# One program, two instruction orders: new ordering constants for a fused cross-attention and feed-forward kernel

## The chip, the core and the metric

The kernel runs on one core of one Trainium2 chip. The metric is the device time of one launch in microseconds (us). TensorE (PE in the profile) does the matrix products and writes them to PSUM, VectorE (DVE), ScalarE (ACT) and GpSimd (POOL) do the elementwise work, and all transfers are issued from SyncE's queue (SP). Each engine runs its own instructions strictly in the order in which the program lists them, and waits on semaphores for what other engines produce. So the order of each engine's list is a design choice, and it is the only thing that this change touches.

## The reference, cut to what matters

`x` has the shape (8, 1024, 512), the context (8, 64, 512), all in float32.

```python
# 1: cross-attention with 16 heads of 32, over 64 context rows
q = layernorm(x) @ Wq.T + bq;  k = ctx @ Wk.T + bk;  v = ctx @ Wv.T + bv
q, k = rotate(q, phase), rotate(k, phase)          # one angle per head
x = x + softmax(q k^T / sqrt(32)) v @ Wo.T + bo
# 2: feed-forward: three cycles of a gated twist
y = layernorm(x)
gf = global_net(y.mean(over the 1024 rows))        # 512 -> 256 -> 128 -> 1
out = y
for _ in range(3):
    tf = coupling_net(out)                         # 512 -> 512 -> 256 -> 128 -> 1, gelu, sigmoid
    out = out + (0.1 + ar * (0.7 * gf + 0.3 * tf - 0.5) * 2) * twist(out)
x = x + out
```

## The kernel before, in words

The rows of `x` are cut into 16 halves, (b, h) with b = 0..7 and h = 0..1, of 512 rows each. Attention (`attn_qx`, `attn_half`) goes over the 16 halves, and then the feed-forward (`ffn_load`, `ffn_part`) over 18 parts: 14 whole halves, and the last two halves cut into two parts of 256 rows each. The names of the tiles carry these numbers: `op_3_0_2` is the third output product of half (3, 0), `l2_7_1_2_0` the second layer of the part of half (7, 1) that starts at row tile 2, in cycle 0. The profile leaves the numbers out (`op`, `l`).

What one attention half does on TensorE, in the order of its data: `xp` turns the normalized rows (16 transposes), `qp` is the query product, `sp` the scores from which VectorE takes the row maxima into `mw`, `mp` turns those, `sT` (two of them) makes the scores again and transposed and takes the maxima off by a small product with `hsel`, ScalarE takes the exponential into `pT` and VectorE clamps it, `dn` (two) sums the denominators, their reciprocals go through DRAM and come back spread over the partitions (`rb`), `ap` (two) is the weighted sum of the values, VectorE multiplies it by `rb`, `aT` is its split, and `op` is the output product, which VectorE adds to the rows `xb`. The rows go to DRAM (`x2d`), the second normalization (`xnf`) is turned by VectorE (`tn`) and goes to DRAM too (`xnd`), and its sum is gathered on GpSimd (`acc`) and reduced by the product `gs`.

A feed-forward part loads its turned rows (`fxn`), splits them (`fxT`; GpSimd forms their sum `fs` for the third of them), makes the products `K`, `A`, `B` with the three weights `wg`, and goes three times through the layers `l2`, `l3`, `l4`. The row of gates that `l4` leaves passes through DRAM to be spread (`c0r`, `ber`, `alr`); VectorE forms the next input `f` from the results of `A` and `B`. At the end (`fin`), ScalarE and VectorE form the output rows from `x2d` (`xt`, `x`).

Large float32 products are made as three products of split operands in the type fp32r: "high by high, high by low, low by high" (`mm3`). In this text these are called **split products**. Other float32 products run plain, each as two passes: `sT`, `dn`, `ap`, `gs`, `l4`, and the layers of the last part's cycles 1 and 2. These are called **plain blocks**. The small `hsel` product at the end of an `sT` is of the type fp32r; with its `sT` it is counted here as one plain block.

No instruction is issued while the kernel is written down. Every call is recorded as an operation with an engine, a cost from a small table, its tiles and its dependencies (class `Plan`; `Engine.__getattr__` records, and line 346 issues later, which is why the profile gives line 346 to nearly everything). `Plan.schedule` then fills the engines' lists as a list scheduler: of the operations that are ready on an engine, it takes the one with the lowest priority number for which buffers are free. The number is the place in the source plus offsets from four tables, by the stage's name, its half or part, and its place from the end:

```python
            op.prio = op.n + SHIFT.get(name, 0) + LAST.get(part, 0)
            op.prio += NEAR.get((name, op.unit), 0)
            op.end_prio = op.prio + TAIL.get((name, part), 0)
...
                    key=lambda op: (op.prio if now < FINALE else op.end_prio)
...
                    busy += CHANGE[op.plain] if op.plain != plain else 0.0
```

`CAPS` limits how many buffers of a kind may be in use at once, and so how far ahead a stage may run. PSUM has 8 banks (room `bank`), which all products share, SBUF has rooms of 8 KB (`r8`, one), 4 KB (`r4`, 36) and 2 KB (`r2`, 16) per partition. `tn` and `fxn` share the one room `r8`.

Of the kernel before, what the change touches and what calls it, by code (L numbers as in the profile page):

```python
# [32 lines left out]
DIRECT, DIRECT2 = 2, 6  # L33
POOLED = 99
PLAIN = [(1, 1), (1, 2)]
CAPS = {'xb': 9, 'wn': 5, 'bv': 1, 'bo': 1, 'jm': 1, 'rt': 1, 'kbd': 2, 'vbd': 2, 'pT': 14, 'acc': 76, 'w3': 3, 'w2f': 1, 'w3f': 1, 'h2': 23, 'w4': 1, 'gw2': 1, 'gw3': 1, 'fxn': 2, 'fs': 9, 'f1': 52, 'AB': 35, 'f2': 6, 'f3': 39, 'c': 97, 'x2': 46, 'xe': 23, 'aT': 20, 'wg': 6, 'w2': 2, 'h1': 25, 'xna': 23, 'xnf': 37, 'xT': 5, 'fxT': 23, 'p': 6, 'sp': 75, 'pp': 2, 'ap': 31, 'op': 126, 'qp': 8, 'xp': 1, 'K': 8, 'A': 16, 'B': 65, 'l2': 16, 'l3': 15, 'l4': 57, 'ct': 3, 'qf': 7, 'qr': 1, 'rb': 13, 'mT': 65, 'mw': 1, 'sT': 43, 'mp': 40, 'dn': 1, 'tn': 2}
PARTS = [1, 1, 1, 1, 1, 1, 1, 1, 1, 1, 1, 1, 1, 1, 2, 2]
LAST = {1: 328, 2: -369, 3: -76, 4: 30, 5: -149, 6: -79, 7: -124, 8: 32}
FINALE = 1170
TAIL = {('A', 1): 231, ('A', 2): 300, ('A', 3): -1159, ('A', 4): 2013, ('A', 5): 815, ('A', 6): -359, ('A', 7): 2233, ('A', 8): -1139, ('B', 1): 459, ('B', 2): 757, ('B', 3): -3031, ('B', 4): -117, ('B', 5): 1537, ('B', 6): 39, ('B', 7): -197, ('B', 8): 2457, ('c0', 1): -1522, ('c0', 2): -4, ('c0', 3): -1115, ('c0', 4): -526, ('c0', 5): 10, ('c0', 6): -755, ('c0', 7): -485, ('c0', 8): -1699, ('c1', 1): -3099, ('c1', 2): 2123, ('c1', 3): -1102, ('c1', 4): -1398, ('c1', 5): -3474, ('c1', 6): -3399, ('c1', 7): 1113, ('c1', 8): -1813, ('c2', 1): 1755, ('c2', 2): 715, ('c2', 3): 236, ('c2', 4): 117, ('c2', 5): 2680, ('c2', 6): 92, ('c2', 7): -1348, ('c2', 8): -2522, ('fin', 1): -571, ('fin', 2): 3573, ('fin', 3): -1695, ('fin', 4): -904, ('fin', 5): -559, ('fin', 6): 1080, ('fin', 7): 238, ('fin', 8): -1451, ('load', 1): -1314, ('load', 2): -1153, ('load', 3): 105, ('load', 4): 689, ('load', 5): 1615, ('load', 6): 1287, ('load', 7): -117, ('load', 8): -775}  # L40
NEAR = {('A', 16): -2012, ('A', 17): -2151, ('A', 19): 54, ('A', 20): -891, ('A', 21): -26, ('B', 16): -109, ('B', 17): -240, ('B', 18): -63, ('B', 19): 528, ('B', 20): 34, ('B', 21): 24, ('av', 0): 34, ('av', 1): -205, ('av', 2): -21, ('av', 12): 143, ('av', 13): -5, ('av', 14): -41, ('av', 15): 450, ('c0', 16): -150, ('c0', 18): -1289, ('c0', 20): -5, ('c0', 21): -45, ('c1', 16): 253, ('c1', 17): 92, ('c1', 18): -42, ('c1', 19): -50, ('c1', 20): -240, ('c1', 21): 12, ('c2', 16): -37, ('c2', 18): 356, ('c2', 19): 90, ('c2', 20): -75, ('c2', 21): 16, ('fin', 17): 94, ('fin', 19): -444, ('fin', 20): -52, ('ln1', 0): -466, ('ln1', 1): 104, ('ln1', 2): -29, ('ln1', 13): 75, ('ln1', 14): 45, ('ln1', 15): 618, ('ln2', 0): 135, ('ln2', 1): -30, ('ln2', 2): 331, ('ln2', 14): -256, ('ln2', 15): -328, ('load', 16): -28, ('load', 17): 256, ('load', 18): 427, ('load', 19): -117, ('load', 21): 36, ('m', 0): -389, ('m', 1): 62, ('m', 2): 46, ('m', 12): -74, ('m', 13): 452, ('m', 14): -61, ('o', 0): 398, ('o', 1): 453, ('o', 2): 40, ('o', 12): -97, ('o', 14): -62, ('o', 15): 65, ('pp', 0): -93, ('pp', 1): 222, ('pp', 2): 25, ('pp', 12): -40, ('pp', 13): 63, ('q', 0): 424, ('q', 1): 45, ('q', 2): 88, ('q', 12): 170, ('q', 13): 1286, ('q', 14): 205, ('q', 15): 1677, ('s', 0): -517, ('s', 2): 6, ('s', 12): -85, ('s', 13): -60, ('s', 14): 263, ('s', 15): -38}
SHIFT = {'A': -269, 'B': -2, 'av': -6048, 'c0': -174, 'c1': 49, 'c2': 353, 'fin': 86, 'ln1': -68, 'ln2': -1598, 'load': -314, 'm': 567, 'o': 106, 'pp': -3220, 'q': 495, 's': -6538}


def ts(i, n):
# [83 lines left out]
class Plan:  # L129
# [110 lines left out]
    def schedule(self):  # L240
        ops = self.ops
        for op in ops:
            name, part = op.stage
# [3 lines that stand above are left out]
        engines = sorted({op.engine for op in ops})  # L247
# [4 lines left out]
        while done < len(ops):  # L252
            for e in engines:
                if free[e] > now:
                    continue
                can = [op for op in ready[e] if op.ready <= now]
                can.sort(
                    key=lambda op: (op.prio if now < FINALE else op.end_prio)
                    + (STICK if e == "tensor" and not op.turn and op.plain != plain else 0)
# [132 lines left out]
def tile_xattn_ffn(  # L392
# [31 lines left out]
    def bank(shape, tag, name):  # L424
        return pl.tile("bank", shape, F32, tag, name, CAPS.get(tag, 8), psum=True)

    def t4(shape, tag, name, dtype=F32):
        return pl.tile("r4", shape, dtype, tag, name, CAPS.get(tag, ROOMS4))

    def t2(shape, tag, name, dtype=F32):  # L430
        return pl.tile("r2", shape, dtype, tag, name, CAPS.get(tag, ROOMS2))

# [961 lines left out]
```

## Time and profile before

| | |
|---|---|
| median of 3 runs | 1293.23 us (1292.69 to 1296.7) |
| the profiled execution | 1292.1 us, of which its span from first to last instruction is 1290.3 us |
| busy in the span | PE 1242.7 us, DVE 1047.4, ACT 873.7, POOL 418.6 |
| 60 to 550 us, attention | PE busy 488.48 of 490 us, DVE 352.25, ACT 288.26 |
| 550 to 620 us, passage to the feed-forward | PE 62.99 of 70 us, DVE 59.01, ACT 29.45 |
| 730 to 1160 us, feed-forward | PE 414.27 of 430 us, DVE 391.75, ACT 337.44 |
| 1160 us to the end | PE 115.38 of 131 us, DVE 114.94, ACT 110.71 |

A busy TensorE is not a TensorE at its peak: products are pipelined, so one shows 0.39 us of busy time while the next starts 0.23 us after it. The distance from start to start is what counts for the sum, and it depends on what follows what. The granted TensorE clock stands in the profile as a share of full speed, in stretches of 1.0 and 0.5; over the span it is 0.987.

### The profile page before, as it was taken

Reading aid. Unit: us, or ns where it says so; the run is one execution under the profiler, and the core shown is the slowest. Engines: PE = TensorE matmul, PEld = TensorE weight load, DVE = VectorE, ACT = ScalarE, POOL = GpSimd, SP = SyncE. Lnnn points to the kernel's source line nnn. Section 1 sums busy time; section 2 is a strip of 40 time slices with the busy share of each in tenths; the row PEclk is TensorE's granted clock in tenths of the full one; section 3 lists DMA queues with packets and bytes.
Section 4 is the critical chain, followed back from the end, with each engine's and each line's share of the span. In section 5 each row is a group of like instructions: output and inputs, shape, how many; then the busy total and the mean of one; then the engine's idle time right before and its main releaser. Section 6 shows DMA issues by size and latency. Waiting matters only on the chain. (4 is left out here: it accounts for less than half of the span.)

```text
span 1290.3 us, 21392 instructions
## 1 busy us (share of the span) xinstructions
PE 1242.7 (96%) x7827; PEld 949.9 (74%) x7827; DVE 1047.4 (81%) x1655; ACT 873.7 (68%) x1520; POOL 418.6 (32%) x463
## 2 busy tenths in 40 slices
PE   7999999999999999998999998999999999999996
PEld 6877777676767677756877786777777777778885
DVE  7856877777777776679777989999899996988997
ACT  4574656555566654535657777878778777788897
POOL 4231434334344333304320412313322320334355
PEclk9999999999999999998999998999999999999998
DMA  7312444443444444353430341246534334243445
GB/s 245 123 35 89 126 140 131 135 119 113 121 123 117 139 136 116 92 140 119 145 81 11 111 148 66 80 122 215 169 104 135 113 116 123 74 131 124 160 148 196
DMA packets 163393, 159.05 MB, mean 123 GB/s; under 512 B 88540, under 2 KB 115416, under 8 KB 163288
## 3 DMA queue, kind: packets, MB, share of 16 engines
q1 hardware_dynamic: 163288, 157.69, 40.2%
q8 instruction: 61, 1.00, 0.3%
q14 instruction: 44, 0.36, 0.1%
HBM read 105.62 MB, written 52.03 MB: 122 GB/s over the span
## 5 line engine op out<-in xcount | busy, mean ns | idle before, releaser
L346 PE MATMUL l<-h,w2H 128*128 128x512 f32 (+1 forms) x832 | 245.5, 379 | 5.5 <-DVE h L346 3.9
L346 PEld LDWEIGHTS l<-h,w2H 128*128 128x128 f32 x832 | 150.6, 191 | 37.8 <-DVE h L346 6.2
L346 PE MATMUL l<-h,w2L 128*128 128x512 f32 (+1 forms) x416 | 155.3, 373 | 0.0
L346 ACT ACTIVATE f<-l,bcol 128x512 f32<-128x512 f32 (+1 forms) x162 | 100.6, 637 | 39.7 <-PE l L346 38.6
L346 DVE TENSOR_TENSOR h<-f,h 128x1024 fp32r<-128x1024 f32 x84 | 105.5, 1263 | 11.8 <-ACT h L346 11.4
L346 POOL TENSOR_TENSOR pc<-cc,rs 128x4 f32<-128x4 f32 (+1 forms) x18 | 27.8, 1545 | 262.2 <-DMA cc<-ber 228.8
L346 ACT ACTIVATE xnf<-xb,sm 128x512 f32<-128x512 f32 x64 | 46.0, 720 | 93.3 <-DVE sm L346 88.2
L346 DVE SCALAR_TENSOR_TENSOR xb<-op,xb 128x512 f32<-128x512 f32 x64 | 43.8, 687 | 76.8 <-PE op L346 76.6
L346 POOL TENSOR_TENSOR xb<-xb,bo_b 128x512 f32<-128x512 f32 x64 | 82.9, 1323 | 56.1 <-ACT xna L346 50.3
L346 POOL TENSOR_TENSOR fs<-fxn 128x512 f32<-128x512 f32 x28 | 53.0, 1911 | 142.7 <-PE l L346 73.4
L346 POOL TENSOR_TENSOR acc<-acc,xnf 128x512 f32<-128x512 f32 x64 | 87.7, 1371 | 31.6 <-ACT xnf L346 28.1
L346 ACT CAST h<-f 128x1024 fp32r<-128x1024 f32 x84 | 87.5, 1048 | 10.7 <-PE l L346 4.8
L346 PEld LDWEIGHTS l<-h,w2L 128*128 128x128 f32 x416 | 79.2, 190 | 13.6
L346 ACT ACTIVATE f<-f,bcol 128x512 f32<-128x512 f32 x112 | 76.5, 719 | 16.9 <-DVE f L346 16.5
L346 DVE TENSOR_REDUCE mw<-sp 128x8 f32<-128x512 f32 x128 | 83.7, 680 | 5.1 <-PE sp L346 4.9
L346 POOL TENSOR_TENSOR rs<-rs,mhalf 128x4 f32<-128x4 f32 x16 | 17.2, 1076 | 199.1 <-DVE rs L346 189.9
L346 ACT ACTIVATE pT<-sT 128x512 f32<-128x512 f32 x128 | 66.3, 621 | 10.6 <-PE sT L346 8.2
L346 DVE TENSOR_TENSOR f<-f,A 128x1024 f32<-128x1024 f32 x56 | 70.1, 1255 | 0.4
L346 ACT ACTIVATE xt<-xt,fa 128x256 f32<-128x256 f32 x128 | 65.3, 594 | 6.3 <-DVE fa L346 6.2
L346 ACT ACTIVATE xna<-xb,mb_a,rs_a 128x512 f32<-128x512 f32 x64 | 47.5, 808 | 16.5 <-DVE mb_a L346 16.4
L346 POOL TENSOR_TENSOR rs_a<-rs_a,mhalf 128x4 f32<-128x4 f32 x16 | 22.7, 1420 | 106.9 <-DVE rs_a L346 93.5
L346 DVE TENSOR_SCALAR pT<-pT 128x1024 f32<-128x1024 f32 x64 | 44.2, 699 | 15.9 <-ACT pT L346 15.7
(414 smaller groups left out, 3612.5 us busy)
## 6 DMA issues: line engine op xcount, KB each, us to landing
xb<-in_x_dram SPq DMA_DIRECT2D x32, 512.0 KB
rb<-rd SPq DMA_DIRECT2D x128, 128.0 KB
x2d<-xb SPq DMA_DIRECT2D x32, 512.0 KB
xnd<-tn_f SPq DMA_DIRECT2D x128, 128.0 KB
x<-x2d SPq DMA_DIRECT2D x32, 512.0 KB
xt<-x2d SPq DMA_DIRECT2D x64, 256.0 KB
out_dram<-x SPq DMA_DIRECT2D x32, 512.0 KB
fxn<-xnd SPq DMA_DIRECT2D x28, 512.0 KB
```

Source lines behind the costliest of these rows:

```text
L346: f(*map(real, args), **{k: real(a) for k, a in kw.items()})
```

## The change

Only constants change: `CAPS`, `LAST`, `FINALE`, `TAIL`, `NEAR` and `SHIFT`. No call, tile, cost or dependency of the kernel's source is touched. The shorter tables:

```diff
-LAST = {1: 328, 2: -369, 3: -76, 4: 30, 5: -149, 6: -79, 7: -124, 8: 32}
-FINALE = 1170
+LAST = {1: 202, 2: -902, 3: 253, 4: 25, 5: -160, 6: -84, 7: -123, 8: 28}
+FINALE = 1150
...
-SHIFT = {'A': -269, 'B': -2, 'av': -6048, 'c0': -174, 'c1': 49, 'c2': 353, 'fin': 86, 'ln1': -68, 'ln2': -1598, 'load': -314, 'm': 567, 'o': 106, 'pp': -3220, 'q': 495, 's': -6538}
+SHIFT = {'A': -269, 'B': -2, 'av': -6588, 'c0': -176, 'c1': 49, 'c2': 352, 'fin': -1, 'ln1': -2616, 'ln2': -2261, 'load': -326, 'm': 586, 'o': -898, 'pp': -2635, 'q': 514, 's': -7454}
```

`TAIL` (56 entries) and `NEAR` (82 before, 88 after) get new numbers throughout. In `CAPS`, 34 limits change; among them `xp` goes from 1 to 5, `qr` from 1 to 7, `rb` from 13 to 5, `vbd` from 2 to 1, `fs` from 9 to 1.

Both built programs hold the same instructions on every engine (6536 products and transposes on TensorE, 1591 instructions on VectorE, 1456 on ScalarE, 466 on GpSimd, 759 transfers). 4829 of TensorE's 6536 stand in the same order. The feed-forward's middle is almost untouched: runs of 693, 371 and 602 TensorE instructions, from part (1, 1) to part (6, 0), are the same one after the other, and there the other engines' lists agree as well. What moves is the attention, the passage from attention to feed-forward, and the last three or four parts.

In the attention's steady part, from the first `op` of half (3, 0) to the first `op` of half (4, 0), TensorE's list reads as follows (R: split products; xp, mp: transposes; the other names: plain blocks):

```
before: R | dn | R | dn | R | xp | R | xp | R | xp | R | xp | R | ap ap | mp | R | sT | R | sT | R |
        dn | R | dn | R | xp | R | xp | R | xp | R | xp | R | ap ap | mp | gs | R | sT | R | sT
after:  R | mp | R | sT | R | sT ap ap dn | R | dn | R | xp | R | xp | R | xp | R |
        mp | R | sT | R | sT ap ap dn gs dn | R | xp | R | xp
```

## The prediction

> **What bounds the kernel now.** I read the page first: which engine is busy, and where.
>
> ```profile
> PE 1242.7 (96%) x7827; PEld 949.9 (74%) x7827; DVE 1047.4 (81%) x1655; ACT 873.7 (68%) x1520; POOL 418.6 (32%) x463
> ...
> PEclk9999999999999999998999998999999999999998
> ```
>
> TensorE is busy 96% of the span, and the clock shows only a few dips. The table of windows splits this: attention (60 to 550 us) has 488.48 of 490 us busy, so nothing is to be won there by removing waits, and only the products' spacing can shrink. In the feed-forward TensorE is idle for 4% and VectorE is busy for 91%, so the two share the bound. After 1160 us VectorE is busy for 114.94 of 131 us.
>
> Next, the waits of TensorE over the whole span, longest in total first:
>
> ```profile
> PE B_0p L346 <- DVE fxT L346: 7.9, 5, 3.2
> PE l L346 <- ACT f L346: 7.6, 7, 1.4
> PE l L346 <- DVE h_0L L346: 4.4, 6, 1.4
> PE tr_cT L346 <- POOL dsel L346: 4.3, 1, 4.3
> PE l L346 <- DVE h L346: 3.9, 4, 2.1
> ```
>
> Most are waits for VectorE in the feed-forward, of about a microsecond each. The longest, 3.2 us, is in the passage. All TensorE waits over 0.1 us sum to 35.2 us behind a start at 4.25 us, and 7.9 us follow its last product. The chain that ended last shows only the final 33 us, so I do not use it.
>
> Last, the timeline of TensorE, for what a change of kind costs. First a plain block between split products, then transposes between them (start, duration):
>
> ```profile
> 341.36 0.39 PE L346 MATMUL op<-wo_0L,aT_0H 128*128 128x512 f32 x1
> 341.59 0.40 PE L346 MATMUL op<-wo_0H,aT_0L 128*128 128x512 f32 x1
> 341.92 1.08 PE L346 MATMUL dn<-pT,dsel 128*32 128x128 f32 x32
> 342.93 0.50 PE L346 MATMUL op<-wo_1H,aT_1H 128*128 128x512 f32 x1
> 343.26 0.39 PE L346 MATMUL op<-wo_1L,aT_1H 128*128 128x512 f32 x1
> 343.50 0.39 PE L346 MATMUL op<-wo_1H,aT_1L 128*128 128x512 f32 x1
> ```
>
> ```profile
> 327.90 0.39 PE L346 MATMUL qp<-xT_a_0H,wq_0L 128*128 128x512 f32 x1
> 328.13 0.60 PE L346 MATMUL xp_a<-ident,xna 128*128 128x128 f32 x4
> 328.49 0.48 PE L346 MATMUL qp<-xT_a_1H,wq_1H 128*128 128x512 f32 x1
> 328.80 0.40 PE L346 MATMUL qp<-xT_a_1L,wq_1H 128*128 128x512 f32 x1
> ```
>
> Split products start 0.23 us apart (341.36 to 341.59). The last one before the plain block takes 0.33 (to 341.92), the first one after it takes 0.33 (342.93 to 343.26), and the next 0.24. So each visit to a plain block from split products costs 0.10 + 0.10 + 0.01 = 0.21 us beyond its own work. The durations hide this: 0.39 to 0.50 us overlap.
>
> **Part 1, fewer visits to plain blocks.** In the built order I counted the places where a split product is followed by a plain block, with transposes passed over. Before there are 127, after 104. Up to the first product of the feed-forward it is 73 against 48: in the attention's steady part two halves have 10 visits before and 5 after, because `ap` and `dn` now stand directly behind the second `sT`, and `gs` between two `dn`. In the last stage there are 3 more (22 against 19), and 1 fewer in between. Sum: 23 x 0.21 = 4.8 us. TensorE has no idle time in attention that could swallow it, so it lies on the path.
>
> **Part 2, fewer runs of transposes.** 86 runs before, 57 after. In the second fence four transposes take 0.36 us and the product behind them 0.31 instead of 0.23: 0.44 us for four. In longer runs they start 0.109 us apart, so a run's edges cost little; with the next product's 0.24 it is some 0.03 us per run, 29 x 0.03 = 0.9 us. Bounds: 0 and 1.7 (twice that).
>
> **Part 3, the passage.** Before, `B_0p` waits 3.23 us for the low half of `fxT`, and the clock then falls. The window of the low clock (length, then busy time of TensorE, its weight loads, VectorE, ScalarE and GpSimd, then the mean clock), and the waiting product in the timeline:
>
> ```profile
> 602.48:612.70 10.22, 6.99 (x19) 5.16 (x18) 10.20 (x13) 5.77 (x10) 3.57 (x4) 0.67 0.27 59
> ```
>
> ```profile
> 607.05 0.79 PE L346 MATMUL B_0p<-fxT,wg_2H 128*128 128x512 f32 x1 [3.23 <-DVE fxT L346]
> ```
>
> In these 10.22 us VectorE is busy for 10.20, TensorE for 6.99, at a mean clock of 0.67: 6.8 us at half speed, which cost 3.4 us. After, `K` comes first and `B` last, and all of `op` of half (7, 1) stands ahead. `K` needs the third `fxT` split, VectorE's later one. Counted from the start of the last `ap` (586.92), that split ended at 610.66, 23.7 us later. In the new list VectorE has two additions of 0.61 us to `xb` more ahead of it, and one `wg` split of 0.60 fewer: 24.4. TensorE's own work up to the reading product is, by the same rows, 1.9 (`ap`) + 5.5 (24 `op`) + 4.2 (18 `op`) + 0.9 wait and 0.95 (`gs`) + 6.9 (30 `op`) + 0.2 = 20.6. So a wait of 3.8 us in `K_0p` takes the place of 3.2 us in `B_0p`, with the same work done on either side. The clock decides the rest: -3 us if it does not fall, +4 if it falls and the `B` weights come late too. I take -0.5, near the row of before. Behind the waiting `K` stand `A`, `B` and the first `l2`; nothing else waits for those at that point but VectorE, which is the late one.
>
> This clock rule needs a word. The Trainium skill ("TensorE: Matmul & The Clock Gate", "What's actually happening") says that half clock follows at least one idle window of about 3.4 us. By that rule a wait of 3.8 us may hold no whole window and the passage would gain 3 us. This case's trace speaks against it: half clock followed a wait of 2.04 us at 1110.75, and here one of 3.23.
>
> GpSimd slows VectorE in the same stretch, and I assume it does so after too: two forms of one `w1c` instruction took 0.68 and 1.77 us (both at 599.38 to 601.76) while GpSimd added `fs` from 599.40 to 602.91. The Trainium skill ("Advanced Engine Details and Errata", "Mode Summary") has them block each other on a shared port. The `acc` and `fs` additions stand beside the same weights in the new list.
>
> **Part 4, the last parts.** The order up to some 1160 us is the old one, so its waits stay and everything comes earlier by parts 1 to 3. In the last 130 us all is new. VectorE sat idle for 2.01 us at 1161.6 (gates from DRAM), 1.55 at 1168.4 (a buffer that `l2` of half (5, 1) held) and 1.97 at 1190.5 (`fxT`); the new list finishes that `l2` ahead of the `B` and `K` of the last halves, which can free up to 1.55. The waits of TensorE for `f` there sum to 4.0 us, and the last plain chain stood nearly alone. Now the last two parts end side by side: the two final `l4` are neighbours, so behind the last product ScalarE has 8 `xt` where it had 4. One pass of eight took 4.05 us at 1275.23, so 2.0 us are added. Gains up to 1.55 + 4.0 against losses of 2.0 and more queueing on VectorE: bounds -4 and +5, taken 0, since nothing says which outweighs.
>
> **Part 5, at nothing.** New places of transfers in SP's queue (loads of `xb`, spreads of `rb`, stores of `xnd`): the old trace has no TensorE wait for a transfer in attention, and `dn` to `ap` has 29 us in the new steady part against 22 before. If that cover went, one half would lose what its transfer is late by. The head's reordered transposes fill a wait of 0.78 us for `xna`: at most -0.6, taken 0.
>
> **Sum.** -4.8 - 0.9 - 0.5 + 0 = -6.2 us. The profiled execution took 1292.1 (span 1290.3), 1.1 below the median; -6.2 on it gives 1285.9, on the median 1287.0.
>
> **Rivals.**
>
> *Late VectorE in the joined blocks (slower).* The block `sT ap ap dn` puts four clamps (0.60 each, start to start), four multiplications (0.60), two `aT` splits (1.14) and the reciprocal (0.87) into one burst of 8 us, where before `ap` and `dn` were 4 to 10 us apart. Walking one half by these spacings, the second `dn` has about 1.0 us to spare, the `aT` split 0.95, `mp` 0.5. If VectorE slips past these, each of some 12 halves pays. To be slower by over 0.3%, 10.1 us are needed, 0.84 us in each half. For it: the row of before where this sequence stood without filler (554.9 to 567 us) shows waits of 0.26 to 0.64 us and a fall of the clock. Against it: in attention VectorE is busy for 352 of 490 us, and only 1.3 us of waits for it showed from 60 to 550. Fully paid, at 1 us per half, it gives 1287 + 12 = 1299.
>
> *Given back in the passage and at the end (the same).* `K_0p`'s wait with the clock's fall (+4) or a worse tail (+4) takes back most of 5.7: about 1292.
>
> *The end closes up (faster still).* If the idle time of VectorE at the end goes and TensorE's waits for `f` go with it: -4, some 1282.
>
> *It does not do what it says.* The counts of 127 and 104 are in the built order, so this is excluded.
>
> **Chances.** The forecast, including the closing end, 0.65; given back 0.18; late VectorE 0.17. 0.3% of the time is 3.9 us, about what a measurement of this kernel can tell from no change: faster means below 1289.3, slower above 1297.1. Range: 1278 (all bounds good: -5.7 - 0.8 - 3 - 4 - 0.6 = -14) to 1298 (late VectorE nearly paid in full); about 0.15 lies above and 0.05 below.
>
> **What would show it.** Right: the first `K` product starts some 5 us earlier than 613.67; TensorE's attention windows stay over 99% busy; two halves take 68.5 us where `op` of (3, 0) to (4, 0) took 69.6. Part 3: a wait of 3 to 4 us at `K_0p` instead of `B_0p`, with half clock behind. Part 4: after the last product 10 us instead of 7.9. Wrong: waits `dn <- DVE pT`, `op <- DVE aT` or `mp <- DVE mw` of over 0.8 us in each half, or clock dips inside the attention.

## The result, and the profile after

The changed kernel took 1301.87 us (median of 5 runs, 1299.45 to 1304.96), the kernel before, run beside it, 1294.73 (1292.69 to 1296.75): ratio 1.0052, 95% interval 1.0034 to 1.0071. It is slower, and above the predicted range. The profiled execution took 1302.1 us, its span is 1300.3; that is 10.0 us over the profiled execution of before, which was one of its quicker ones.

The page's line of busy times and the clock row, as shown of before:

```profile
PE 1238.4 (95%) x7827; PEld 958.4 (74%) x7827; DVE 1048.0 (81%) x1655; ACT 874.4 (67%) x1520; POOL 417.5 (32%) x463
...
PEclk9999999999999999999999998999999999898998
```

TensorE is busy for 4.3 us less in a span that is 10 us longer: its products do stand closer, and the time went into waiting. Where, shows in the windows (length, then busy time of TensorE, its weight loads, VectorE, ScalarE and GpSimd, then the mean clock, the DMA share and GB/s), first of before, then of after:

```profile
60.00:550.00 490.00, 488.48 (x3800) 346.89 (x3802) 352.25 (x652) 288.26 (x514) 179.29 (x139) 1.00 0.40 115
1160.00:1290.00 130.00, 115.38 (x788) 102.30 (x786) 114.94 (x221) 110.71 (x246) 58.38 (x76) 0.97 0.49 158
```

```profile
60.00:550.00 490.00, 482.25 (x3863) 352.54 (x3862) 360.66 (x658) 289.97 (x516) 188.42 (x138) 1.00 0.41 114
1160.00:1300.00 140.00, 121.58 (x802) 107.78 (x802) 119.45 (x228) 113.93 (x251) 40.30 (x76) 0.93 0.47 148
```

In the attention TensorE now has 7.8 us of idle time, where it had 1.5. VectorE is busy for 8.4 us more in this window, with six instructions more; 5.4 us of it are five clamps that take longer, shown below. Over the whole span it is busy for only 0.6 us more. At the end the mean clock is 0.93, and it was 0.97. The waits of TensorE, first two rows of before, then the rows of after:

```profile
PE xp_a L346 <- ACT xna L346: 1.1, 2, 0.8
...
PE dn L346 <- DVE pT L346: 0.8, 3, 0.3
```

```profile
PE l L346 <- ACT f L346: 15.7, 7, 3.9
PE l L346 <- DVE h_0L L346: 6.1, 8, 1.4
...
PE dn L346 <- DVE pT L346: 4.0, 6, 0.8
PE xp_a L346 <- ACT xna L346: 3.2, 6, 0.8
PE K_0p L346 <- DVE fxT L346: 2.6, 1, 2.6
PE gs L346 <- POOL acc L346: 2.5, 3, 1.2
...
PE B_0p L346 <- ACT B__12412 L346: 2.1, 1, 2.1
```

The 3.2 us of `B_0p` in the passage became 2.6 us of `K_0p`; the forecast was 3.8. Grown are `dn` and `xp_a` in the attention (4.0 and 3.2 us, from 0.8 and 1.1) and, at the end, the waits for ScalarE.

Start times of the same product in each profile show where a kernel gains and loses (us from the span's start; the rows of the experiments are explained below):

| profile | second `sp` of half (7, 1) | first `B`, part (1, 1) | first `K`, part (7, 0) | end of TensorE | span |
|---|---|---|---|---|---|
| before | 554.9 | 729.4 | 1139.3 | 1282.4 | 1290.3 |
| after | 555.8 | 730.9 | 1143.2 | 1291.4 | 1300.3 |
| s1: new attention, old end | 554.5 | 733.4 | 1143.7 | 1286.9 | 1294.8 |
| s2: old attention, new end | 554.9 | 729.0 | 1142.5 | 1290.4 | 1299.4 |
| b1: new order, short bias addition | 549.6 | 728.9 | 1139.2 | 1285.3 | 1294.2 |
| x2: new order, clamp first | 549.3 | 723.8 | 1135.1 | 1281.8 | 1290.8 |
| s1x2: new attention, clamp first, old end | 549.7 | 723.9 | 1137.2 | 1280.2 | 1288.1 |
| q1: s1x2, sums early in the passage | 549.4 | 730.8 | 1142.2 | 1286.0 | 1293.7 |
| q2: s1x2, sums early at the end | 549.5 | 725.4 | 1133.1 | 1276.3 | 1284.2 |

So the changed kernel arrives at the end of the attention 0.9 us late instead of 5 to 6 early (s1, with the same lists there, 0.4 us early), and from the first `K` of part (7, 0) to the end of TensorE it takes 148.2 us instead of 143.1. Each place has a cause of its own. A row is one execution, so a difference of a few us in one column can be chance; the last section shows two such chances.

**In the attention**, the timeline of the changed kernel around one half (4, 1), VectorE, GpSimd and TensorE in turn:

```profile
376.63 2.37 DVE L346 TENSOR_SCALAR pT<-pT 128x1024 f32<-128x1024 f32 x2
377.04 4.34 POOL L346 TENSOR_TENSOR xb<-xb,bo_b 128x512 f32<-128x512 f32 x3 [1.23 <-ACT xna L346]
379.05 0.64 PE L346 MATMUL dn<-pT,dsel 128*32 128x128 f32 x16 [0.72 <-DVE pT L346]
382.64 0.87 PE L346 MATMUL xp_a<-ident,xna 128*128 128x128 f32 x6 [0.49 <-ACT xna L346]
```

The two clamps of `pT` should take 1.29 us. The second one starts at 377.23, GpSimd's addition of the bias to `xb` 0.19 us before it, and that clamp takes 1.77 us instead of 0.69. The half's second `dn` waits 0.72 us for it, and the next `xp_a` 0.49 us for ScalarE, which had waited for VectorE. The same happens at 170, 239, 308, 377 and 446 us, once in each pair of halves. Before, no clamp of these halves took over 0.70 us; the additions there began behind the last clamp (timeline of before, VectorE and GpSimd):

```profile
308.94 0.69 DVE L346 TENSOR_SCALAR pT<-pT 128x1024 f32<-128x1024 f32 x1
309.95 5.04 POOL L346 TENSOR_TENSOR xb<-xb,bo_b 128x512 f32<-128x512 f32 x4 [1.12 <-ACT xna L346]
```

**At the end**, GpSimd, ScalarE, VectorE and TensorE at 1224 us:

```profile
1216.33 4.18 POOL L346 TENSOR_TENSOR pc<-cc 128x4 f32<-128x4 f32 x2
1222.09 1.40 POOL L346 TENSOR_TENSOR fs__12820<-fxn 128x256 f32<-128x256 f32 x2
1223.53 0.62 ACT L346 CAST fxT<-fs__12820 128x512 fp32r<-128x512 f32 x1 [2.81 <-POOL fs__12820 L346]
1224.18 0.69 DVE L346 TENSOR_TENSOR fxT<-fs__12820,fxT 128x512 fp32r<-128x512 f32 x1 [2.59 <-ACT fxT L346]
1224.57 0.64 PE L346 MATMUL l<-f,w4b 128*32 128x128 f32 x4 [2.69 <-ACT f L346]
```

The sum `fs` of the last part stands behind the 12 small gate instructions of part (6, 1) in GpSimd's list. These have 128 x 4 elements and can take 0.2 us each, but two of them took 4.18 us while VectorE ran one subtraction or addition behind the other. So `fs` is late, then its cast on ScalarE, then everything that ScalarE has behind the cast, then TensorE. Before, this `fs` stood ahead of that group (GpSimd's timeline of before):

```profile
1199.35 1.55 POOL L346 TENSOR_TENSOR fs__12619<-fxn 128x256 f32<-128x256 f32 x2 [9.55 <-DMA fxn<-xnd]
1217.62 10.77 POOL L346 TENSOR_TENSOR pc<-cc,rs 128x4 f32<-128x4 f32 x1 [16.72 <-DMA cc<-ber]
```

There a single gate instruction took even 10.77 us, with VectorE busy without a break beside it, but the last `fs` was done before.

### The profile page after: what moved, and what is told of

It is laid out like the page before. It is cut to its first block, busy times and chain, and to the rows that moved or that the text cites. A ratio compares the mean times of both kernels' runs of the same rounds, so it can differ in the third digit from the quotient of the medians.

```text
span 1300.3 us, 21383 instructions
## 1 busy us (share of the span) xinstructions
PE 1238.4 (95%) x7827; PEld 958.4 (74%) x7827; DVE 1048.0 (81%) x1655; ACT 874.4 (67%) x1520; POOL 417.5 (32%) x463
## 5 line engine op out<-in xcount | busy, mean ns | idle before, releaser
L346 POOL TENSOR_TENSOR xb<-xb,bo_b 128x512 f32<-128x512 f32 x64 | 95.1, 1513 | 75.3 <-ACT xna L346 67.7
L346 POOL TENSOR_TENSOR pc<-cc,rs 128x4 f32<-128x4 f32 (+1 forms) x18 | 9.8, 544 | 281.1 <-DMA cc<-ber 211.8
L346 POOL TENSOR_TENSOR fs<-fxn 128x512 f32<-128x512 f32 x28 | 50.0, 1806 | 143.1 <-DMA fxn<-xnd 76.6
L346 DVE TENSOR_REDUCE mw<-sp 128x8 f32<-128x512 f32 x128 | 81.0, 679 | 2.0 <-PE sp L346 1.9
L346 DVE TENSOR_SCALAR pT<-pT 128x1024 f32<-128x1024 f32 x64 | 48.6, 777 | 21.1 <-ACT pT L346 21.0
L346 ACT ACTIVATE qf<-qp,bqr 128x512 f32<-128x512 f32 x64 | 42.9, 681 | 22.3 <-PE qp L346 21.9
```

What stands on the lines that cost most here:

```text
L346: f(*map(real, args), **{k: real(a) for k, a in kw.items()})
```

## The experiments

**Which part of the order loses?** Both kernels hold the same instructions one after the other in the feed-forward's middle, so the lists can be cut there and joined. The cut is where the sets of what stands before it agree, on every engine:

```diff
+        one, two = self.lists(ONE), self.lists(TWO)
...
+            forced[e] = a[:k] + b[k:]
+        return self.schedule(ONE, forced)
```

> The lists of every engine are those of the changed kernel up to the feed-forward's middle (where both kernels hold the same instructions one after the other) and those of the kernel before from there on. Theory (VectorE and GpSimd block each other, and both ends of the program lose by it): the changed kernel reached the first B product of part (1, 1) at 730.86 us against 729.39 before, so this one should be 1.5 us slower than the kernel before, some 1296, with the clamps beside GpSimd's additions still at 1.77 us. Rival 1 (all of the loss is in the last 130 us and attention is gained as forecast): 5 us faster, 1290. Rival 2 (the attention's waits are the whole loss): 7 us slower, 1302.

Measured: 1296.07 us (median of 12 runs) against 1295.48 (35 runs), ratio 1.0006 (0.999 to 1.0022).

> The reverse: the lists of the kernel before up to the feed-forward's middle, those of the changed kernel from there on. Theory: the end of the changed kernel costs 4.9 us after 1143 us and 1.1 us behind the last product, so 6 us slower than before, some 1301; 9 us if GpSimd is held up at 1102 us again as in the profile of the changed kernel. Rival 1: 12 us slower (the whole loss and the gain of attention with it). Rival 2: no change, 1295.

Measured: 1300.38 us, ratio 1.0041 (1.0021 to 1.0061). So the new end costs 5 us, and the new attention gains nothing. The two effects together, 1.0047, are the changed kernel's 1.0052 within the intervals. Rivals 1 and 2 are both out. In s2's profile the last `fs` was not late (ScalarE waited 0.1 us for it at 1221.6); the long wait there is that of `B_0p` for ScalarE, 3.05 us at 1195, behind another late `fs` (2.5 us). So the row at 1224 us is one form of this loss and not all of it.

**Is it the bias addition beside the clamp?**

```diff
-            pl.gpsimd.tensor_tensor(v, v, bo_b, ALU.add)
+            cut = lambda a: a[:, :8]
+            pl.gpsimd.tensor_tensor(v.via(cut), v.via(cut), bo_b.via(cut), ALU.add)
```

> The changed kernel with GpSimd's additions of the output bias to the rows xb cut to 8 of 512 columns (the rest of the bias is left out), all else in the same order. Theory (the last clamp of every second half stands beside one of these additions and waits for it): the five clamps of 1.77 us fall to 0.69, the waits of dn for pT (0.72) and of xp for xna (0.49) go, which is 1.2 us in each of 6 pairs of halves, so 7 us faster than the changed kernel: some 1295. Rival (the clamp is late because ScalarE's exponentials are, since sT ap ap dn stand in one block): the waits stay, 1302.

Measured: 1296.41 us, ratio to the kernel before 1.0007 (0.9989 to 1.0026). The five clamps fell to 0.69 us, the waits of `dn` for `pT` in the steady halves are gone, those of `xp_a` fell from 0.49 to 0.35, and two halves took 68.03 us (`op` of (3, 0) to (4, 0)) instead of 69.07. The attention's end came 5.3 us earlier than before, but in this profile the first `B` of part (1, 1) only 0.5 us: the passage took the rest, most of it by a lower clock, as the last section shows.

> The kernel before with the same cut, as the control. Theory: no clamp stood beside these additions, and the attention showed 1.3 us of waits for VectorE in all, so at most 1 us faster than before: some 1294. Rival (the additions slow the whole program through their share of the memory): several us faster, as with the changed order.

Measured: 1295.27 us, ratio 0.9995 (0.9979 to 1.0012). In the old order the additions cost nothing, so it is their place in the new order that does. But the edit also shortened GpSimd's work, so the next one only moves it:

```diff
+            def look(col=col):   # ahead of GpSimd's first bias addition of half (b, 1)
+                self.nc.gpsimd.tensor_tensor(self.spare.get(), col.get(), col.get(), ALU.add)
+            op.calls = [look] + op.calls   # col: 4 columns of the last clamped pT of (b-1, 1)
```

> The changed kernel, in which GpSimd reads four columns of the last clamped pT of half (b-1, 1) ahead of its first bias addition of half (b, 1), for the five halves in which the two stood side by side; nothing else moves. So the additions come some 2 us later and behind the clamp. Theory (a lock, not a lack of time: the additions need only begin after the clamp): the five clamps take 0.69 us instead of 1.77, dn waits for pT no more there, two halves take 68.0 us instead of 69.07, as with the shortened additions; the passage takes part of it, so some 1297 in all. Rival (with the additions late, the next wait comes up behind them: xb for op, or rs_a on GpSimd): two halves stay at 69 us or more, 1302.

Measured: 1293.86 us, ratio 0.9983 (0.9964 to 1.0002), where the changed kernel had 1.0052. The timeline of this kernel at the same place (VectorE, GpSimd, VectorE; the file is longer, so the recorded line has another number):

```profile
372.16 1.29 DVE L356 TENSOR_SCALAR pT<-pT 128x1024 f32<-128x1024 f32 x2
373.53 0.20 POOL L323 TENSOR_TENSOR spare<-pT 128x4 f32<-128x4 f32 x1 [2.19 <-DVE pT L356]
373.68 6.99 POOL L356 TENSOR_TENSOR xb<-xb,bo_b 128x512 f32<-128x512 f32 x4
377.22 2.30 DVE L356 TENSOR_TENSOR aT_1L<-rb,aT_1H 128x1024 fp32r<-128x1024 f32 x1
```

Both clamps take 1.29 us together, and GpSimd's additions, all of them still made, wait 2.19 us for them. Two halves take 68.05 us. The additions now hold up a later subtraction instead (`aT_1L`, 2.30 us for 1.21), which TensorE does not wait for. So it is a block and not a lack of time, and what it costs depends on whom it meets. The rival, another wait coming up in its place, is out. The time is some 3 us better than the theory's 1297, which counted on a loss in the passage.

> New attention with the clamp first, from the feed-forward's middle on the lists of the kernel before. Theory: 5 us are gained up to 550 us against the kernel before, the passage gives most of it back, as it did with the shortened additions (there the first B product of part (1, 1) came 0.5 us earlier than before), the end is the old one: 1292 to 1295, no change or just faster than before. Rival (what the passage took was bad luck with the clock, not VectorE): 1290.

Measured: 1289.05 us, ratio 0.9956 (0.9937 to 0.9975). This beats both kernels by more than expected: the passage did not take the gain here (5.5 us at the first `B` of part (1, 1)). It is the rival's number (1290), and the rival's reason, the clock, is borne out by the profiles in the last section. The same program again:

> The best version once more, unchanged. Theory: 0.4 to 0.5% faster than the kernel before, as in its first run. Rival (that ratio was the luck of one chip or of its clock): no difference from the kernel before.

Measured: 1291.71 us against 1294.6, ratio 0.9965 (0.9947 to 0.9983). The gain stands.

**Is the end's loss the wait for GpSimd's sums?**

```diff
-        pl.scalar.copy(xT[0][0], s)
-        low(xT[0][1], s, xT[0][0])
+        near = s.via(lambda a: f32(xT[1][0]).get())
+        pl.scalar.copy(xT[0][0], near)
+        low(xT[0][1], near, xT[0][0])
```

> Old attention with new end, in which the third split fxT is made from the first split's high half instead of from GpSimd's sum fs; GpSimd still forms fs, and the order is the same, so only the wait for GpSimd is taken out (the value of fs is left out of the products K). Theory (the new end loses because its sums fs stand where GpSimd is kept from its port, and ScalarE and TensorE queue behind): the wait of B_0p for ScalarE's B (3.0 us) and the half clock behind it go, and what is left against the old end with the same edit is the 1 to 2 us behind the last product: some 1294. Rival (the order of ScalarE and VectorE is the loss, whoever forms the sum): still 5 us slower than the old end with the same edit.

Measured: 1290.15 us, ratio 0.9963 (0.9947 to 0.9979).

> The kernel before with the same edit, as the control. Theory: the waits of B_0p for fxT (7.9 us in sum) that come from late sums go, at 1110.75 us (2.04 and 1.7 of half clock) above all: 2 to 4 us faster than before, some 1292. Rival: no change, since VectorE is the bound there.

Measured: 1290.61 us, ratio 0.9976 (0.9955 to 0.9997). Without the wait for the sums the new end is no slower than the old one: 1.0041 against 1 became 0.9963 against 0.9976. The wait is the whole loss that the runs can tell. The 1 to 2 us behind the last product that I expected to be left stand in the profiles (9.2 us against 7.9), but not in the medians.

If the place in GpSimd's queue does it, moving the sums alone must help:

```diff
+            held = [
+                i for i, o in enumerate(order[:x])
+                if o in op.deps or any((b.room, b.slot) in slots for b in o.bufs)
+            ]
+            order.insert(max(held) + 1, order.pop(x))   # op: a sum fs; slots: its buffer
```

> The changed kernel, with GpSimd's sums fs of the last two parts moved up in GpSimd's own list: fs of part (7, 1) at row tile 2 from behind the 12 small gate instructions (pc and rc) of part (6, 1) to before them, fs of (7, 1) at row tile 0 three places up. Theory (the new end loses because these sums queue behind small instructions that wait for the port): the idle time of ScalarE and VectorE for fs at 1223.5 us (2.8 and 2.6 us) and TensorE's wait of 2.7 us there with its half clock (1.7 us) go, the wait at 1194.5 shrinks: 4 us faster than the changed kernel, some 1298. Rival (VectorE's backlog at the end is the loss, the sums are late because everything is): no change, 1302.

Measured: 1298.43 us, ratio 1.002 (1.0002 to 1.0037), against 1.0052 for the changed kernel. ScalarE no longer waits for the last part's `fs`; TensorE's waits around 1222 to 1224 us fell from 2.7 to 1.0 us. The wait of `B_0p` for ScalarE's `B` stayed (2.4 us at 1197, 2.1 at 1194 in the changed kernel). It goes the way of the theory and is as large as it said, though the two intervals touch.

> New attention with the clamp first, old end, and in GpSimd's list every fs as early as its loads allow (six parts move, by 2 to 9 places). Theory: in the old end the last sum already stands ahead of the gates, so little is left to gain: 1287 to 1289. Rival (late sums cost the middle too): 1284.

Measured: 1294.99 us, ratio 0.9997 (0.998 to 1.0014): a miss to both sides. The attention still ended early in the profile (549.7 us), but the gain was gone by the first `B` of part (1, 1) (731.4).

> The kernel before with its sums as early as its loads allow (six parts move). Taking the wait for the sums out altogether made it 0.24% faster, which is the most that this can give: 1292 to 1295 by the theory. Rival (GpSimd, ahead in the queue, takes the port from VectorE at worse moments): slower, 1297.

Measured: 1293.63 us, ratio 0.9979 (0.9966 to 0.9992), as the theory said. In the profiles of both, the product `gs` of batch 6 came 3.4 us later behind the `op` ahead of it than without the edit. So the two sums in the passage were tried alone, and then those at the end alone:

> The best version so far (new attention, clamp first, old end) with the sums fs of the first two parts alone moved up in GpSimd's list, the two that stand in the passage. Theory (in the passage GpSimd's additions acc, which the product gs needs, are the more urgent ones; put behind fs they cost what the earlier run with all sums early lost): gs of batch 6 starts 3.4 us later than without the edit, and the whole gain of the attention goes: 1295. Rival (the loss of that run came from the parts in the middle): 1289.

Measured: 1295.87 us, ratio 1.0014 (0.9998 to 1.003). TensorE's longest row of waits in that kernel:

```profile
PE gs L427 <- POOL acc L427: 11.5, 3, 6.8
```

With two sums put ahead of GpSimd's additions `acc`, `gs` waits 11.5 us for them in all, and the gain of the attention goes.

> The best version with the sums of parts (6, 1) and (7, 1) alone moved up. Theory: the gain of 2 to 3 us that the old order had from this edit between 1095 and 1140 us comes on top of the attention's, 1286 to 1288. Rival (the early sums are no gain anywhere): 1289 or later.

Measured: 1287.73 us (median of 7 runs) against 1294.6, ratio 0.9948 (0.993 to 0.9966): the lowest median of all. Its interval overlaps those of the two runs without the early sums (0.9956 and 0.9965), so what these sums add is not shown by the times. In the profile it took 407.6 us from the first `B` of part (1, 1) to the first `K` of part (7, 0), where s1x2 took 413.2. This version has the new attention with five small GpSimd instructions that hold the bias additions back, the old end, and two sums a few places up.

**Is TensorE's longest wait at the end worth anything?** In the changed kernel the last product waits 3.93 us, since ScalarE does 8 `xt` of part (6, 1) first:

```profile
1285.92 4.04 ACT L346 ACTIVATE xt<-xt,fa 128x256 f32<-128x256 f32 x8 [0.17 <-DVE fa L346]
...
1290.38 1.02 PE L346 MATMUL l<-bcol,f 128*128 128x1 f32 x4 [3.93 <-ACT f L346]
...
1291.59 4.26 ACT L346 ACTIVATE xt<-xt,fa 128x256 f32<-128x256 f32 x8
```

```diff
+        late = {o for o in order[:last] if made(o, "xt_6_1_0")}   # and all that depends on them
+        first = [o for o in order[: last + 1] if o not in late]   # last: the second c behind the last l4
+        order = first + [o for o in order if o in late] + order[last + 1 :]
```

> The changed kernel with the last chain (f, and the two c behind the last l4) put ahead of the eight xt of part (6, 1) in ScalarE's list, and these xt with what hangs on them behind it. Theory (at the end ScalarE has 16 xt of 0.49 us to do whatever the order): TensorE's last wait of 3.93 us goes, but the span ends at most 1.2 us earlier, what ScalarE is idle between; no change in the time that can be measured, some 1301. Rival (the wait is on the path): 4 us faster, 1298.

Measured: 1305.05 us, ratio 1.0066 (1.005 to 1.0082). The wait is gone and no time is won; from the last product's end to the span's end it is now 13.9 us instead of 9.0. ScalarE's lines in this kernel:

```profile
1291.08 4.03 ACT L354 ACTIVATE xt<-xt,fa 128x256 f32<-128x256 f32 x8
1296.01 4.28 ACT L354 ACTIVATE xt<-xt,fa 128x256 f32<-128x256 f32 x8 [0.90 <-DVE fa L354]
```

The 16 `xt` set the end, whatever stands ahead of them. Putting the short chain first only leaves ScalarE idle while it waits for TensorE.

## Why the prediction was wrong, step by step

**Parts 1 and 2 (-5.7 us) had the mechanism right; that the size came out so well is partly luck.** With the clamp out of the way the attention ended 5.2 to 5.6 us earlier than before. But two halves took 68.05 us, 1.5 us less than the 69.57 of before, where 1.1 less were forecast (68.5), and they did so with a wait of 0.35 us of `xp_a` still in them. So at the second `sp` of half (5, 1) x2 stood 7.7 us ahead of before, and at that of (7, 1) 5.6: the last halves gave 2 us back, 1.0 of it where that `sp` waits 1.6 us for VectorE's `qr` (0.6 before). The counts hold. Part 2's 0.03 us per run does not come out of its own rows: 0.44 us for four against 4 x 0.109, with 0.01 for the next product, is 0.01 per run, 0.4 us in all.

**What failed first is the sentence that this gain "lies on the path", since TensorE had no idle time to swallow it.** It then made its own: a wait of 0.72 us and one of 0.49 in each pair of halves, and the pair took 69.07 us instead of 68.05. At the second `sp` of half (5, 1) the changed kernel was still 2.3 us ahead of before, at that of (7, 1) 0.9 behind. This is the place of the rival "late VectorE in the joined blocks" but not its mechanism. I looked for a burst too long for VectorE, and gave the second `dn` about 1.0 us to spare. The burst fits; a single clamp came 1.08 us late and `dn` waited 0.72, so the room was 0.36. I had read GpSimd's blocking of VectorE in the passage, from two forms of `w1c` (0.68 and 1.77 us), and did not ask where the new lists put GpSimd's other additions. Part 5 went through SP's queue and left GpSimd's out. Holding the additions back was worth 0.4 to 0.5% in the version with the old end (1.0006 to 0.9956 and 0.9965): this is what had turned the gain into nothing.

**Part 3 (-0.5 us) was near.** The wait moved from `B_0p` to `K_0p` as said, 2.6 us where 3.8 were forecast. From the `gs` of batch 6 to the first `B` of part (1, 1) it took 130.5 us against 129.9, with new waits for GpSimd's `acc` (1.2) and of the product `gp` (1.8). In the other profiles of the new lists it is 131.0 to 133.1 (without q1 and p1, which put the sums ahead of `acc`), in s2 and b2 with the old ones 130.9 and 130.7. By the medians, 131.4 against 130.7, 0.7 us were lost and not 0.5 gained.

**Part 4 (0, between -4 and +5) was mis-sized.** It measured +5 us by the joined lists of s2, the far end of its own bounds. I had listed the idle times of VectorE that could close and the `xt` that could be added, and nothing on GpSimd: that TensorE would wait for a sum behind the gates is not in the working. "Nothing says which outweighs" was not so: the place of `fs` in GpSimd's list was there to be compared. The tail forecast at 10 us after the last product was 9.0.

By measured terms the new attention with the old end is 0.06% or 0.8 us slower, which is the forecast's -5.7 for the spacing and, by subtraction, 6.5 for the clamps, what they hold up and the passage; the new end adds 5.3 (0.41%). That makes 6 us, where 6.7 (0.52%) were measured for both.

Of the signs named ahead, TensorE's attention window is 98.4% busy instead of over 99%, and the row `dn <- DVE pT` is there, but with 0.72 us in every second half, less than the 0.8 in each that was to mean "wrong". The sign of being right came true all the same: the first `K` started at 608.23 us, 5.4 earlier. `K` now stands ahead of `B`, so this start could not tell the gain. Half clock behind `K_0p`'s wait did not come in the changed kernel's profile.

## What to carry to other kernels

When an order changes, compare every engine's list, the idle ones' too: GpSimd was busy for a third of the time and decided the sign here. Some VectorE and GpSimd instructions exclude each other from start to end (here clamps, `aT_1L` and other instructions with two inputs in SBUF), so place GpSimd's work beside VectorE work that nobody waits for, and what another engine needs soon ahead of GpSimd's small gate instructions; but not ahead of what is needed sooner still, as `acc` was. A wait is worth what its end would release: with the 0.72 us of `dn` went 1.0 us of each pair of halves, with the 3.93 us at the end nothing.

## What the runs showed of the hardware

The block works in both directions, and not fairly. A gate instruction on GpSimd of 128 x 4 elements, which takes 0.2 us by itself, took 7.08 us in the changed kernel and 10.77 in the one before, while VectorE went from one two-input instruction to the next without a break; one clamp, the other way round, took 1.08 us more. Not every VectorE instruction is held up: beside the additions at 309.95 us (before) its reciprocal from PSUM took 0.96 us and its addition of a PSUM result 0.68, as elsewhere. The same pair of GpSimd's instructions in the old trace, then in the new one (timeline of before, timeline of after):

```profile
1101.33 0.35 POOL L346 TENSOR_TENSOR pc<-pc,mb 128x4 f32<-128x4 f32 x2
```

```profile
1102.32 7.23 POOL L346 TENSOR_TENSOR pc<-pc,mb 128x4 f32<-128x4 f32 x2
```

The lists are the same there, and all engines are 0.99 us later; presumably it differed which engine got in first, and ScalarE then waited 4.3 us for `fs`. In 12 profiles the instructions and lists are the same here: nine have the 7.08 us, and three (before, s1, b1) have not. From the first `B` of part (1, 1) to the first `K` of part (7, 0) the nine took 411.2 to 413.8 us, the three 409.9 to 410.4. So 1 to 4 us between executions go with this chance, and the profile of before is one of the lucky ones. The Trainium skill ("SBUF — State Buffer", "SBUF: two separate sides") has the shared port as an exclusive lock between GpSimd's instructions and those of VectorE that run in a two-port mode or have two inputs in SBUF, taken by whoever starts first for the whole instruction. The clamp's 1.77 us agree with that: it was held until the addition of 1.40 us was over.

The same wait is followed by half clock in one execution and not in another. `K_0p` waits the same time in the changed kernel and in s1, whose lists are the same up to there (timelines of after, then of s1):

```profile
611.24 0.50 PE L346 MATMUL K_0p<-fxT,wg_0H 128*128 128x512 f32 x1 [2.62 <-DVE fxT L346]
611.58 0.40 PE L346 MATMUL K_0p<-fxT,wg_0L 128*128 128x512 f32 x1
```

```profile
611.16 0.54 PE L408 MATMUL K_0p<-fxT,wg_0H 128*128 128x512 f32 x1 [2.61 <-DVE fxT L408]
611.49 0.63 PE L408 MATMUL K_0p<-fxT,wg_0L 128*128 128x512 f32 x1
```

At full clock a product takes 0.40 us, in the other profile 0.63. Half clock came in stretches of 3.4, 6.8 or 10.2 us in all profiles, apart from the one that runs into each program's end; from 550 to 730 us it sums to 6.8 us in the changed kernel's and to 20.5 in that of s1. That is 6.8 us of difference in TensorE's work between two executions of the same lists. From the second `sp` of half (7, 1) to the first `B` of part (1, 1), 3.8 us of it show (178.9 against 175.1).

Most of what the passage took in b1 is this chance. From the second `sp` of half (7, 1) to the `gs` of batch 6 its TensorE list is the one of x2, and the windows differ in the clock (b1, then x2):

```profile
549.60:596.83 47.23, 44.39 (x327) 27.48 (x327) 34.86 (x59) 16.80 (x27) 7.83 (x6) 0.89 0.55 158
```

```profile
549.26:592.48 43.22, 39.96 (x327) 26.75 (x327) 34.51 (x59) 16.70 (x27) 7.83 (x6) 1.00 0.58 169
```

b1 had 10.2 us at half clock here and x2 none, and b1 took 4.0 us longer, of the 5.1 by which it reached part (1, 1) later. The other profiles agree, old lists or new, where `fs` was not put ahead of `acc`: 43.2 to 43.7 us without half clock, 44.6 with 3.4 us of it, 45.8 to 46.0 with 6.8, 47.2 with 10.2.
